# A row-by-row norm on ScalarE and earlier adds in a graph layer on one core

## The chip, the cores and the metric

The kernel runs on one core of one Trainium2 chip. The metric is the device time of one execution in microseconds (us), as the median of several runs. A core has five engines with a program each: TensorE (PE; its weight loads are shown as PEld), VectorE (DVE), ScalarE (ACT), GpSimd (POOL) and SyncE (SP), which here only issues transfers. They wait for each other by semaphores.

## The reference

One layer of a graph network: 6250 nodes of 64 features, 206250 edges sorted by their target `dst`.

```python
h = jnp.maximum(_layernorm(x, axis=-1), 0.0)
msg = h[src] + edge_attr_64
agg = jax.ops.segment_sum(msg, dst, num_segments=6250)
x = x + (jax.nn.relu(agg @ W1 + b1) @ W2 + b2)
```

## The kernel before, in words

**The norm (the head).** x lies in SBUF as `xl`, 49 rows of 64 elements on each of 128 partitions, in two parts of 24 and 25 rows (`parts`, split at `XA`). Mean, centred x, variance and `rs`, one over the root, are worked out for both parts. Then `norm_h(k)` (L550) takes the maximum with 0 and scales, in one VectorE instruction over the whole part (L552), and stores it on SP into `table`, a copy of h in HBM (L553); `norm_copy(k)` (L555) copies the part on ScalarE into `h2`, the operand of the later matmuls, and `norm_low(k)` adds its low half there.

**Most edges: counts.** For windows of edges TensorE multiplies two one-hot arrays (`hot_lo`, `hot_key`, made by VectorE in `count`, L837, for three steps at once in two buffers) into `pc` in PSUM: how often each node of a table of 128 x 49 occurs as a source (L847). ScalarE moves these counts into a ring in SBUF (L850). `multiply` (L866) then multiplies h2 with the counts into `pv`, the sums of h per target node, and `add_products` (L879) adds them into `agg` (called `sums` in the profile). `pc` has two buffers, so the matmuls of a step wait for ScalarE's reading of two steps before.

**The other work.** The edges' own features are summed with one-hot matmuls into `bank` (`chunk_hot` L422, `chunk_sum` L434) and placed into `pv` (L450). For 18 groups of edges at the end of the list h is not counted but gathered: POOL gathers rows of `table` with indirect transfers that add onto the edge features (`pfeat`, L296); `sum_groups` (L477) sums a pair of groups, `place_groups` (L489) puts it into place, ScalarE copies it to `sum_p` (L491), and `add_sums` (L461) adds it on VectorE, in two instructions at addresses read at run time, into `agg`. Nodes whose sums are complete go through the layers: `mlp_hidden` multiplies agg with W1 into `ph` (L915, ScalarE's `hid` L917), `mlp_product` gives `po` (L922), then the residual is added (L933) and stored.

**The order.** It is written out by hand: each engine gets its instructions in the order in which the Python code emits them. After the head there are 23 blocks of 14 steps (block b, step s, number n = 14 b + s). Each step emits one `count`, for block b - 1 a part of `multiply`, and what is due: the dictionary `before` gives things for a step number, and `at(n, f)` puts f to the end of step n. `mlp` puts ph of one set of nodes to step 8 of a block, and of another to step 11 where there is one (`LAYERS`). A pair of groups that is summed at step n (only at `GROUPS`, steps 0, 1, 2 and 4) is placed at the next step in `PLACED` that is at least 2 later; `add_later` puts its adds at least 5 steps behind that (3 in the last block), at any step but 10 (`ADDED`). The conditions on agg are kept by semaphores: an instruction that writes agg at a run-time address waits for matmuls before it in the order that read agg, and matmuls wait for adds before them.

**The part of the head around the change.** `norm_scale` gives rs; `unpack_pair(0)`, `chunk_rows`, `chunk_columns` (it ends with ScalarE's `cols`, L360), `turn_pair(0)` (it ends with ScalarE's `keys`, L705, which the first hot_lo waits for), two of `by_quarters` (ScalarE's `src_p`, L632), `norm_h(0)`, `norm_copy(0)`, `chunk_index`, gathers of `dstq` and words on POOL, `load(0)` (two transfers of features on SP), `norm_h(1)`, `norm_copy(1)`, `load(1)`. At step 4 `chunk_nodes(0)` works on the gathered dstq on VectorE (L378) and `chunk_turn(0)` turns it on TensorE (`pdst`, L386); step 3 has the last `by_quarters`, step 7 the `seek` on ScalarE (`inrow`, L312).

Of the kernel before, what the change touches and what calls it, by code (L numbers as in the profile page):

```python
# [14 lines left out]
AF = mybir.ActivationFunctionType  # L15
# [4 lines left out]
P = 128  # L20
# [45 lines left out]
HI = 49  # L66
# [6 lines left out]
XA = 24  # L73
# [3 lines left out]
NW = 23  # L77
# [33 lines left out]
KR = 540  # L111
AHEAD = 16
OPENING_US = 15.0


@with_exitstack
def gnn_kernel(ctx: ExitStack, tc: tile.TileContext, x, src_t, dst_t, dst_g, edge, w1, b1, w2, b2, out):
    nc = tc.nc
# [12 lines left out]
    table = dram.tile([HI * P, D], F32, name="table")  # L131
# [209 lines left out]
    def chunk_rows(c0, c1):  # L341
        s = starts[:, c0:c1]
        nc.vector.tensor_scalar(s, s, float(G * P * J - CE), None, op0=OP.min)
        nc.vector.tensor_copy(starts_i[:, c0:c1], s)
# [59 lines left out]
    def load(u):  # L404
        if u >= len(units):
            return
        _, c, n = units[u]
        at = nc.values_load_multi_w_load_instructions(
            starts_i[0:1, c:c + n], engines=[mybir.EngineType.SP], min_val=0, max_val=G * P * J - CE,
            skip_runtime_bounds_check_because="sums of edges before, at most that by a min")[1]  # L410
        feats[u] = [work.tile([P, CT, D], F32, name="feat", bufs=4) for _ in range(n)]
        for k in range(n):
            nc.sync.dma_start(feats[u][k].rearrange("p (q k) d -> p q (k d)", q=JQ),
                              edge[ds(at[k], CE), :].rearrange("(q p k) d -> p q (k d)", p=P, k=JP))
# [86 lines left out]
    xh = xl[:, :HI, :]  # L501
    stat = late.tile([P, 4, HI], F32, name="stat")
    mean, var, rs, t = (stat[:, k, :] for k in range(4))
    parts = [(0, XA), (XA, HI)]
# [14 lines left out]
    def wide(a, h0, h1):  # L519
        return a[:, h0:h1].unsqueeze(2).to_broadcast([P, h1 - h0, D])  # L520
# [21 lines left out]
    def norm_scale():  # L542

        nc.vector.reciprocal(rs, t)
        nc.vector.tensor_tensor(t, rs, rs, op=OP.mult)
        nc.vector.tensor_tensor(t, t, var, op=OP.mult)
        nc.vector.tensor_scalar(t, t, -0.5, 1.5, op0=OP.mult, op1=OP.add)
        nc.vector.tensor_tensor(rs, rs, t, op=OP.mult)

    def norm_h(k):  # L550
        h0, h1 = parts[k]
        nc.vector.scalar_tensor_tensor(xh[:, h0:h1], xh[:, h0:h1], 0.0, wide(rs, h0, h1), op0=OP.max, op1=OP.mult)  # L552
        nc.sync.dma_start(table.rearrange("(l h) d -> l h d", l=P)[:, h0:h1, :], xh[:, h0:h1])  # L553

    def norm_copy(k):  # L555
        h0, h1 = parts[k]
        nc.scalar.activation(h2[:, h0:h1, :D], xh[:, h0:h1], AF.Copy)
# [66 lines left out]
    def by_quarters(t0, t1):  # L624
        rows = src_s.bitcast(F32)
        for t in range(t0, t1):
            own = slice(t * QP, (t + 1) * QP)
            px = ps.tile([P, 512], F32, tag="pv", name="psrcq")[:, :GP * PK]
            for b in range(PQ):
                nc.tensor.matmul(px, spread[own, b].rearrange("p a c -> p (a c)"), rows[own, :, b, :],  # L630
                                 start=(b == 0), stop=(b == PQ - 1))
            nc.scalar.activation(src_p[:, :, t], px.rearrange("p (g k) -> p g k", k=PK), AF.Copy)  # L632
# [43 lines left out]
    def unpack(i0, n, p, base):  # L676
        words = words_of.pop(i0)
        klo = late.tile([P, 2, SLOTS], I32, name="klo")
        khi = late.tile([P, 2, SLOTS], I32, name="khi")
        nc.vector.tensor_scalar(klo[:p, :n], words[:p, :n], P - 1, None, op0=OP.bitwise_and)  # L680
        nc.vector.tensor_scalar(khi[:p, :n], words[:p, :n], LO_BITS, None, op0=OP.logical_shift_right)
        klof = late.tile([P, 2, SLOTS], BF16, name="klof")
        nc.scalar.activation(klof[:p, :n], klo[:p, :n], AF.Copy)
        khif = late.tile([P, 2, SLOTS], BF16, name="khif")
        nc.vector.tensor_tensor(khif[:p, :n], khi[:p, :n], base.unsqueeze(2).to_broadcast([p, n, SLOTS]),
                                op=OP.subtract)
        unpacked[i0] = klof, khif
# [4 lines left out]
    def turn(i0, n, p, cols):  # L692
        klof, khif = unpacked.pop(i0)
        pk = ps.tile([P, 2, 2, P], F32, tag="po", name="pk", bufs=1)
        for i in range(n):
            nc.tensor.matmul(pk[:, 0, i, :p], klof[:p, i, :], identb[:p, :p], start=True, stop=True)
            nc.tensor.matmul(pk[:, 1, i, :p], khif[:p, i, :], identb[:p, :p], start=True, stop=True)
        pk = pk.rearrange("s k i p -> s k (i p)")
        for a, z, col in cols:
            while a < z:  # L700
                m = min(z - a, KR - col % KR)
                assert col + m - KR <= opened[0], (i0, col, m, opened[0])
                for c in range(col, col + m):
                    at_col[c % KR] = c
                nc.scalar.activation(keys[:, :, col % KR:col % KR + m, :],  # L705
                                     pk[:, :, a:a + m].unsqueeze(3).to_broadcast([P, 2, m, 2]), AF.Copy)
                a, col = a + m, col + m
        rows = min(p, NWIN - i0 * P) if i0 < IC and n == 1 else p
        kept[i0] = khif, n, rows
# [7 lines left out]
    def unpack_pair(i0):  # L717
        n = min(2, IC - i0)
        unpack(i0, n, P, nbase[:, i0:i0 + n])

    def turn_pair(i0):
        n = min(2, IC - i0)
        end = min(n * P, NWIN - i0 * P)
        mid = min(max((SB + 1) * BT - NX - i0 * P, 0), end)
        turn(i0, n, P, [(a, z, i0 * P + a + o) for a, z, o in ((0, mid, 0), (mid, end, NX)) if a < z])
# [266 lines left out]
    by_quarters(0, 1)  # L992
    norm_scale()
    unpack_pair(0)
    chunk_rows(0, 2 * RC)
    chunk_columns(0, 2, "pc", 2)
    turn_pair(0)
    by_quarters(1, 3)
    norm_h(0)
    norm_copy(0)  # L1000
# [3 lines left out]
    fetch_dst(1)  # L1004
    fetch_pair(4)
    load(0)
    norm_h(1)
    norm_copy(1)
    load(1)
    open_ring()  # L1010
# [62 lines left out]
    steps = [(b, s) for b in range(NW) for s in range(STEPS)]  # L1073
    first_step = [steps.index((b, 0)) for b in range(NW)]
    last = len(steps)
# [4 lines left out]
    PRODUCTS = (5, 12, 19, 26, 33, 41, HI)  # L1080
    ADDED, LOADED = 10, 2
    LAST, LATE = (5, 10), 9
    GROUPS, PLACED = (0, 1, 2, 4), (1, 2, 4, 5)
    ready = []
    queued = set()
# [21 lines left out]
    def add_later(n):  # L1107

        upto = h_next

        def f():
            add_sums()
            for m in range(NW, NB):
                if (upto >= G or (start[m + 1] + 30) * (E / N) <= upto * P * J) and m not in queued:
                    queued.add(m)
                    ready.append(m)
        at(n, f)

    for n, (b, s) in enumerate(steps):
        for f in before.get(n, []):  # L1120
            f()
        count(b, s)
        if b >= 1 and s < len(PRODUCTS):
            multiply(b - 1, PRODUCTS[s])
        if b >= 1 and s == PLACES:
            for u in places[b - 1]:
                chunk_place(u)
        if b >= 1 and s == (ADDED if b < NW - 1 else LATE):
            add_products(b - 1)
            if b - 1 > SB:  # L1130
                ready.append(b - 1)
        k = n - (first_step[SB + 1] + ADDED + 1)
        if 0 <= k < 3 * -(-NX // 4) and k % 3 == 0:
            add_seconds(k // 3 * 4)
            if k // 3 == -(-NX // 4) - 1:
                ready[:0] = range(SB + 1)
        if s == LOADED or b == NW - 2 and s == STEPS // 2:
            for m in ready[:len(LAYERS)] if b < NW - 1 else ready + [NW - 2, NW - 1]:
                if m not in xs:
                    residual(m)  # L1140
        if b == NW - 1 and s == STEPS // 2:
            for m in range(NW, NB):
                if m not in queued:
                    residual(m)
        if s in (LAYERS if b < NW - 1 else LAST) and ready and ready[0] in xs:
            mlp(ready.pop(0), n)
        for f in later.pop(n, []):
            f()
        if n >= 3:
            if h_next < G and s in GROUPS and fetched.get(h_next + 1, 1e9) + LAND_US <= clock(n):  # L1150
                features_h(h_next)
                n_placed = next((k for k in range(n + 2, last) if b == NW - 1 or steps[k][1] in PLACED), last)
                at(n_placed, place_groups, h_next)
                h_next += GB
                add_later(next((k for k in range(n_placed + (3 if b == NW - 1 else 5), last) if steps[k][1] != ADDED), last))
            if n == 3:
                pool[0] = clock(n - 1) + OPENING_US
            pool_until(clock(n) + LAND_US)
# [142 lines left out]
```

## Time and profile before

| | before |
|---|---|
| median of 3 runs | 478.37 us (478.1 to 478.75) |
| profiled execution, its own time | 481.19 us |
| its span, first to last instruction | 479.4 us |
| TensorE busy | 418.0 us, 87% of the span |
| VectorE busy | 417.1 us, 87% |
| ScalarE busy | 369.0 us, 77% |
| GpSimd busy | 355.8 us, 74% |
| mean granted clock of TensorE | 0.981 |

The profile is one execution, recorded by the hardware. In a timeline a line gives start and length in us, engine, source line, operation, output and inputs by the program's names, shape, how many were merged (x), and in brackets how long the engine sat idle before it and what released it. A line of the waits gives who waited for whom, the sum in us, how many times, and the longest. Busy shares are means over stages with different limits; the head ends at about 60 us, and the blocks' rhythm after that is some 17 to 18 us.

### The profile page before, as it was taken

The page shows a single profiled execution, that of the slowest core. Times are in us where ns is not written, and L with a number is a line of the kernel's source. Part 1 is how long each engine was busy: PE and PEld are TensorE (multiplying, and loading weights), DVE is VectorE, ACT ScalarE, POOL GpSimd, SP SyncE. Part 2 cuts the span into 40 slices and gives each one's busy share as a digit, 9 for nine tenths or more (in the row PEclk, how much of TensorE's full clock was granted, in tenths as well). Part 3 has the DMA queues.
Part 4 walks back from the last instruction along what each step waited for, and adds up shares of the span by engine and source line. Part 5 has one row for each costly group of instructions (what it writes and reads, how often), then busy time and mean ns, then how long its engine had stood idle before and what let it go on. Part 6 is the DMA issues. An engine that isn't in the chain of part 4 may idle for free.

```text
span 479.4 us, 17275 instructions
## 1 busy us (share of the span) xinstructions
PE 418.0 (87%) x7339; PEld 373.4 (78%) x7340; DVE 417.1 (87%) x562; ACT 369.0 (77%) x611; POOL 355.8 (74%) x223
## 2 busy tenths in 40 slices
PE   2147698999988999999979999999999999999974
PEld 2136597887887898898878988988988988888964
DVE  7788989889999899989699899898998899898740
ACT  3636889978878789889868789787887788688650
POOL 7777888898888888888888888888888888500000
PEclk9999699999999999999989999999999999999998
DMA  9949457468367668576674694596695694474330
GB/s 236 219 148 313 118 147 167 98 175 218 66 161 193 155 172 228 121 202 166 152 189 114 178 246 105 142 248 142 147 241 123 158 225 106 130 210 133 91 83 16
DMA packets 120050, 77.70 MB, mean 162 GB/s; under 512 B 32448, under 2 KB 118400, under 8 KB 119744
## 3 DMA queue, kind: packets, MB, share of 16 engines
q1 hardware_dynamic: 97452, 67.13, 47.9%
q0 software_dynamic: 22288, 8.67, 14.1%
q8 instruction: 59, 0.97, 0.9%
q10 hardware_dynamic: 228, 0.75, 0.5%
q14 instruction: 23, 0.19, 0.1%
HBM read 72.53 MB, written 3.99 MB: 160 GB/s over the span
## 4 chain that ended last, share of the span: by engine, by line
PE 70%; ACT 11%; DMA 8%; DVE 6%; issue 3%; POOL 1%; DVEq 0%; ACTq 0%; POOLq 0%
PE pv L866 27%; PE pc L847 23%; PE bank L434 10%; ACT counts L850 8%; PE po L922 3%; DMA rows<-in_dst_g,row_i 2%; DMA feat<-in_edge 2%; PE pv L450 2%; DVE hot_key L837 2%; DMA dstq<-in_dst_g,cols_i 2%; DVE hot_lo L837 1%; POOL rows L296 1%; PE ph L915 1%; ACT junk L673 1%; DMA firsts_i<-in_dst_g 1%
## 5 line engine op out<-in xcount | busy, mean ns | idle before, releaser
L296 POOL DMA_INDIRECT pfeat<-table,src_p x144 | 299.7, 2081 | 45.0 <-issue 39.9
L850 ACT ACTIVATE counts<-pc 128x882 fp32r<-128x882 f32 x322 | 286.2, 916 | 56.7 <-PE pc L847 49.9
L847 PE MATMUL pc<-hot_key,hot_lo 128*128 128x147 bf16 x1932 | 180.8, 232 | 27.1 <-ACT counts L850 16.9
L866 PE MATMUL pv<-counts,h 128*128 128x252 f32 x1127 | 171.6, 292 | 0.1
L847 PEld LDWEIGHTS <-hot_lo 128*128 128x128 bf16 x1932 | 132.2, 100 | 49.2 <-issue 22.9
L837 DVE TENSOR_TENSOR hot_key<-iota_key,keys 128x2664 bf16<-128x2664 bf16 (+1 forms) x109 | 165.5, 1519 | 0.0
L837 DVE TENSOR_TENSOR hot_lo<-iota_lo,keys 128x2304 bf16<-128x2304 bf16 (+1 forms) x109 | 145.6, 1336 | 21.4 <-PE pc L847 18.1
L866 PEld LDWEIGHTS pv<-counts,h 128*128 128x128 f32 x1127 | 143.6, 190 | 0.4 <-ACT counts L850 0.3
L434 PE MATMUL bank<-feat,hot 128*21 128x64 f32 x3288 | 62.4, 225 | 0.2 <-DMA feat<-in_edge 0.2
L434 PEld LDWEIGHTS bank<-feat,hot 128*21 128x21 f32 x3288 | 49.9, 103 | 9.5 <-issue 0.7
L422 DVE TENSOR_TENSOR hot<-rel,iota 128x504 f32<-128x504 bf16 x69 | 46.5, 673 | 0.0
L296 POOL DMA_INDIRECT words<-packed,first_i x15 | 21.2, 1413 | 4.6 <-issue 4.3
L296 POOL DMA_INDIRECT rows<-in_dst_g,row_i x15 | 18.7, 1248 | 5.2 <-issue 3.0
L437 ACT ACTIVATE by_node<-bank 128x128 f32<-128x128 f32 x69 | 19.5, 283 | 2.1 <-PE bank L434 1.9
L879 DVE TENSOR_TENSOR sums<-sums,pv 128x126 f32<-128x126 f32 (+2 forms) x31 | 10.0, 343 | 11.0 <-PE pv L866 10.9
L917 ACT ACTIVATE hid<-ph,b1s 128x252 f32<-128x252 f32 (+2 forms) x25 | 11.6, 463 | 9.0 <-PE ph L915 9.0
L922 PE MATMUL po<-w2s,hid 128*126 128x64 f32 (+2 forms) x100 | 17.1, 295 | 1.2 <-ACT hid L917 1.2
L922 PEld LDWEIGHTS po<-w2s,hid 128*126 128x126 f32 (+2 forms) x100 | 13.8, 198 | 4.3 <-ACT hid L917 2.0
L915 PE MATMUL ph<-sums,w1s 128*128 128x252 f32 (+2 forms) x50 | 16.2, 405 | 0.5 <-ACT y L928 0.4
L450 PE MATMUL pv<-select,by_node 128*64 128x42 f32 x274 | 12.6, 235 | 0.0
L450 PEld LDWEIGHTS pv<-select,by_node 128*64 128x64 f32 x274 | 9.9, 137 | 3.1
L312 ACT ACTIVATE inrow<-rows,nhalf 128x256 bf16<-128x256 int32 x15 | 7.4, 499 | 5.2 <-DMA rows<-in_dst_g,row_i 5.2
(201 smaller groups left out, 244.4 us busy)
## 6 DMA issues: line engine op xcount, KB each, us to landing
feat<-in_edge SPq DMA_DIRECT2D x137, 384.0 KB
pfeat<-in_edge SPq DMA_DIRECT2D x18, 256.0 KB
pfeat<-table,src_p POOLq DMA_INDIRECT x144, 4.4
xl<-in_x SPq DMA_DIRECT2D x2, 768.0 KB
xs<-in_x SPq DMA_DIRECT2D x23, 63.0 KB
out_y<-y SPq DMA_DIRECT2D x23, 63.0 KB
dstn<-in_dst_g SPq DMA_DIRECT2D x1, 1024.0 KB
table<-xl SPq DMA_DIRECT2D x1, 800.0 KB
```

Source lines behind the costliest of these rows:

```text
L296: nc.gpsimd.indirect_dma_start(out=rows, out_offset=None, in_=source, in_offset=bass.IndirectOffsetOnAxis(ap=index, axis=0), compute_op=op)
L422: nc.vector.tensor_tensor(hot_of[u][:, :n].rearrange("p c j w -> p (c j) w"), rel[:, c:c + n].rearrange("p c q k -> p (c q k)").unsqueeze( ...
L434: nc.tensor.matmul(bank[q * QP:q * QP + WQ, i * D:(i + 1) * D], hot[:, i, j, :], feat[i][:, j, :], start=(k == 0), stop=(k == JP - 1))
L437: nc.scalar.activation(by_node[u][:, :n].rearrange("p c d -> p (c d)"), bank[:, :n * D], AF.Copy)
L450: nc.tensor.matmul(pvs[b][0][i * D:(i + 1) * D, a:a + CN], of[:, i, :], select, start=False, stop=False)
L837: nc.vector.tensor_tensor(hot[:, :n].rearrange("p t (m o) -> p t m o", o=2), iota_k.rearrange("p (m o) -> p m o", o=2).unsqueeze(1).to_bro ...
L847: nc.tensor.matmul(pc[:, k, m * K:(m + 1) * K], hot_lo[:, j, :], hot_key[:, j, :K], start=True, stop=True)
L850: nc.scalar.activation(ring[:, (2 * b + half) % 3, :, i * ST * V:(i + 1) * ST * V].rearrange("p h (k m) -> p h k m", k=2), pc[:, :, :ST // ...
L866: nc.tensor.matmul(pv.rearrange("p (k n) -> p k n", k=2), h2[:, h, :], of[:, :, h, :], start=(h == 0), stop=(h == HI - 1))
L915: nc.tensor.matmul(ph[:, :n], w1s, agg[:, start[b]:start[b + 1]], start=True, stop=True)
L917: nc.scalar.activation(outs[b][:, :n], ph[:, :n], AF.Relu, bias=b1s)
L922: nc.tensor.matmul(po[:pairs[b], k, :], outs[b][:, k:2 * pairs[b]:2], w2s, start=True, stop=True)
```

## The change

Two things. In the head the second part of `norm_h`, one VectorE instruction of 128 x 1600, becomes 25 activations on ScalarE of 128 x 64, one for each row: Relu with the row's column of `rs` as the scale. The first 12 are put behind `unpack_pair(0)`, that is ahead of `cols`, the other 13 behind `turn_pair(0)`, that is ahead of the two `by_quarters`. The store of this part stays where it was in SP's order (`norm_store`). And `add_later` puts a pair's adds at least 3 steps behind its placing, at step 6 or 7 of a block alone (in the last block at any step but 9).

```diff
+MID = XA + 12
...
+    def norm_rows(a, z):
+        for h in range(a, z):
+            nc.scalar.activation(xh[:, h], xh[:, h], AF.Relu, scale=rs[:, h:h + 1])
+
+    def norm_store(k):
+        h0, h1 = parts[k]
+        nc.sync.dma_start(table.rearrange("(l h) d -> l h d", l=P)[:, h0:h1, :], xh[:, h0:h1])
...
     norm_scale()
     unpack_pair(0)
+    norm_rows(XA, MID)
     chunk_rows(0, 2 * RC)
     chunk_columns(0, 2, "pc", 2)
     turn_pair(0)
+    norm_rows(MID, HI)
     by_quarters(1, 3)
     norm_h(0)
     norm_copy(0)
...
     load(0)
-    norm_h(1)
+    norm_store(1)
     norm_copy(1)
     load(1)
...
+    ADDS = (6, 7)
...
-                add_later(next((k for k in range(n_placed + (3 if b == NW - 1 else 5), last) if steps[k][1] != ADDED), last))
+                add_later(next((k for k in range(n_placed + 3, last) if steps[k][1] in ADDS or steps[k][0] == NW - 1 and
+                                steps[k][1] != LATE), last))
```

In step numbers, of the nine pairs of adds five move: those at (block, step) (6, 7), (8, 7), (15, 7) and (17, 7) by one step to step 6, and that at (10, 9) by two steps to (10, 7). In block 10 ph stands at step 8.

## The prediction

> **What bounds the kernel now.** I read the page first, then the chain of work that ended last in order of time, then the waits summed over the span, and last the timelines of single engines around the places that the diff touches. From the page, the span and the chain's shares by engine:
>
> ```profile
> span 479.4 us, 17275 instructions
> ...
> PE 70%; ACT 11%; DMA 8%; DVE 6%; issue 3%; POOL 1%; DVEq 0%; ACTq 0%; POOLq 0%
> ```
>
> The reader is to see that the chain lies on TensorE for most of the span: an edit on VectorE or ScalarE counts only where TensorE waits for it. The profiled execution took 481.19 us, 1.8 us more than its span and 2.8 us more than the median of the three timed runs, 478.37 us. The sum below is made against 481.19 us and then carried over to 478.37 us as a difference. About 0.2%, 0.96 us, can be told from no change here.
>
> The two parts of the change touch two places. The first is one long wait of VectorE, from the summed waits:
>
> ```profile
> DVE sums L461 <- PE ph L915: 4.4, 1, 4.4
> ```
>
> It happens once. The timeline of VectorE shows where, and that of TensorE what it did there:
>
> ```profile
> 233.48 0.67 DVE L422 TENSOR_TENSOR hot<-rel,iota 128x504 f32<-128x504 bf16 x1
> 238.54 0.43 DVE L461 TENSOR_TENSOR sums<-sums,sum_p 64x52 f32 x2 [4.39 <-PE ph L915]
> 239.00 1.36 DVE L837 TENSOR_TENSOR hot_lo<-iota_lo,keys 128x2304 bf16<-128x2304 bf16 x1
> 240.27 1.54 DVE L837 TENSOR_TENSOR hot_key<-iota_key,keys 128x2664 bf16<-128x2664 bf16 x1
> ```
>
> ```profile
> 234.37 0.56 PE L847 MATMUL pc<-hot_key,hot_lo 128*128 128x147 bf16 x6
> ...
> 236.26 0.87 PE L434 MATMUL bank<-feat,hot 128*21 128x64 f32 x48
> ...
> 237.80 0.63 PE L915 MATMUL ph<-sums,w1s 128*128 128x252 f32 x2
> 238.27 0.55 PE L847 MATMUL pc<-hot_key,hot_lo 128*128 128x147 bf16 x6
> 241.87 0.56 PE L847 MATMUL pc<-hot_key,hot_lo 128*128 128x147 bf16 x6 [3.05 <-DVE hot_key L837]
> 242.36 1.37 PE L434 MATMUL bank<-feat,hot 128*21 128x64 f32 x48
> ```
>
> L461 is the pair of adds of gathered sums placed at step 9 of block 10. It waits for the matmul ph of step 8, which reads the same array, and ph stands in TensorE's queue behind everything until 237.80. VectorE sits idle for 4.39 us, so hot_lo and hot_key of the next three steps come late, and TensorE, done with 238.27, waits 3.05 us for them. So here VectorE sets the end, and what it waited for was TensorE itself.
>
> **The adds, part by part.** With the change the pairs of adds stand at step 6 or 7 of a block, the last block apart. In the instruction order of the two kernels six of the nine keep their place on VectorE and three pass one small instruction; one of these three is the pair above, which goes ahead of the "hot" at 233.48 and, in the program, ahead of ph. Among the semaphores it waits for TensorE's is gone, and ph waits for the adds instead. From ScalarE's timeline there:
>
> ```profile
> 233.09 0.21 ACT L491 ACTIVATE sum_p<-placed 128x52 f32<-128x52 f32 x1 [0.23 <-PE placed L489]
> ...
> 238.19 0.92 ACT L850 ACTIVATE counts<-pc 128x882 fp32r<-128x882 f32 x1
> ```
>
> sum_p is done at 233.09 + 0.21 = 233.30, before VectorE is free at about 233.5; the adds take 0.43, "hot" 0.67, so VectorE is through at 234.6. ph at 237.80 is far behind them. hot_lo then needs the buffer of two openings earlier, which TensorE frees with the counts at 234.37 + 0.56 = 234.93. hot_lo and hot_key take 1.36 + 1.54 with some overlap: ready near 237.8, before TensorE ends 238.27 + 0.55 = 238.82. What is late next is the bank of counts: ScalarE reads it from 238.19 to 239.11. So the matmuls of 241.87 start near 239.15, 2.7 us sooner.
>
> There is more. From the table by stretches (busy time and count of each engine, then the granted clock, the share of the DMA engines and GB/s):
>
> ```profile
> 244.00:246.00 2.00, 2.00 (x16) 2.00 (x16) 1.46 (x2) 0.79 (x3) 1.70 (x2) 0.51 0.72 195
> ```
>
> TensorE came back slow: the same 48 matmuls took 0.87 at 236.26 and 1.37 at 242.36, and the granted clock was 0.51 from 244 to 246.
>
> [...]
>
> The whole is best read from block to block. These are ph of block 10 (above, 237.80), of block 11, and of two later blocks with no other extra work between them:
>
> ```profile
> 259.03 0.63 PE L915 MATMUL ph<-sums,w1s 128*128 128x252 f32 x2
> ...
> 366.98 0.63 PE L915 MATMUL ph<-sums,w1s 128*128 128x252 f32 x2
> ...
> 384.02 0.63 PE L915 MATMUL ph<-sums,w1s 128*128 128x252 f32 x2
> ```
>
> Block 10 to 11 takes 259.03 - 237.80 = 21.23; the later pair 384.02 - 366.98 = 17.04. The difference is 4.2, the direct count 2.7 plus the slow matmuls. I take 4.1 us off. If the moved adds found their cover gone (VectorE late by more than the 0.3 us that it waits for the buffer anyway), it would cost that lateness alone; all nine pairs together are 18 adds of about 0.2.
>
> **The rows in the head.** The timelines of ScalarE and VectorE there:
>
> ```profile
> 17.79 0.50 ACT L312 ACTIVATE inrow<-rows,nhalf 128x256 bf16<-128x256 int32 x1
> ...
> 28.64 0.23 ACT L540 ACTIVATE stat<-stat 128x49 f32<-128x49 f32 x1
> ...
> 31.99 0.41 ACT L683 ACTIVATE klof<-klo 128x256 bf16<-128x256 int32 x1
> 34.48 0.23 ACT L360 ACTIVATE cols<-pcols 128x2 f32<-128x2 f32 x2 [2.08 <-PE pcols L358]
> 35.02 1.02 ACT L705 ACTIVATE keys<-pk 128x1024 bf16<-128x1024 f32 x1 [0.31 <-PE pk L697]
> 36.87 0.20 ACT L632 ACTIVATE src_p<-psrcq 128x36 int32<-128x36 f32 x1 [0.82 <-PE psrcq L630]
> 37.75 0.21 ACT L632 ACTIVATE src_p<-psrcq 128x36 int32<-128x36 f32 x1 [0.68 <-PE psrcq L630]
> 37.85 2.90 ACT L557 ACTIVATE h<-xl 128x1536 fp32r<-128x1536 f32 x2
> 40.65 1.70 ACT L850 ACTIVATE counts<-pc 128x882 fp32r<-128x882 f32 x2
> ```
>
> ```profile
> 34.96 1.82 DVE L552 SCALAR_TENSOR_TENSOR xl<-xl,stat 128x1600 f32<-128x1600 f32 x1
> ...
> 44.27 0.42 DVE L378 TENSOR_SCALAR dstq<-dstq,cols 128x384 f32<-128x384 int32 x1 [1.87 <-DMA dstq<-in_dst_g,cols_i]
> ...
> 47.29 1.54 DVE L837 TENSOR_TENSOR hot_key<-iota_key,keys 128x2664 bf16<-128x2664 bf16 x1
> ```
>
> One VectorE instruction (the second of L552, 1.82 us at 34.96) is replaced by 25 activations of 128x64 on ScalarE, 12 ahead of "cols" and 13 behind "keys". The store of the second part of the table leaves on SP behind them, near 39.4 us by the sum below, and SP's next loads behind that store; I cost both at nothing, since their readers come steps later, and if that cover is gone it is at most the same 1.65 us as below. Price of one row: 128x49 took 0.23 with no per-partition operand; 64 adds 0.01; the operand (rs, one column) adds what L312 with nhalf shows over L683 without, both 128x256: 0.50 - 0.41 = 0.09. So 0.33 long. Neighbours overlap: 37.75 lasts 0.21 but 37.85 starts 0.10 after it.
>
> So a row takes 0.235 of ScalarE, 25 rows 5.9 us. Bounds: 0.14 if the operand is free, 0.33 if nothing overlaps; I take 0.235, from the nearest rows. The waits named in the brackets between 31.99 and 40.65 are 2.08 + 0.31 + 0.82 + 0.68 = 3.9, and four overlaps that a waiting engine lost give 0.35 more: 4.25 us of cover. The first counts (40.65) come 5.9 - 4.25 = 1.65 us later. The queue behind the rows: cols moves from 34.48 to about 35.2, keys from 35.02 to 35.3, then src_p, the two copies at 37.85, the counts.
>
> Who waits for that? On TensorE, and in ScalarE's next row:
>
> ```profile
> 41.60 0.90 PE L847 MATMUL pc<-hot_key,hot_lo 128*128 128x147 bf16 x6 [0.98 <-ACT counts L850]
> ...
> 44.28 0.92 PE L847 MATMUL pc<-hot_key,hot_lo 128*128 128x147 bf16 x6
> 45.49 0.91 PE L386 MATMUL pdst<-ident,dstq 128*128 128x128 f32 x3 [0.30 <-DVE dstq L379]
> ...
> 48.88 0.95 PE L847 MATMUL pc<-hot_key,hot_lo 128*128 128x147 bf16 x12 [1.00 <-ACT counts L850]
> ```
>
> ```profile
> 47.18 1.71 ACT L850 ACTIVATE counts<-pc 128x882 fp32r<-128x882 f32 x2 [0.25 <-PE pc L847]
> ```
>
> The third group of pc (41.60) is held by the first counts, and what stands behind it goes with it. But two later steps are held by others, which takes up part of the shift. pdst at 45.49 waits for VectorE's dstq, and dstq for its gather; the pc at 44.28 would have let it go at 45.20: 0.3 us of slack. At 48.88 TensorE waits for hot_key (47.29 + 1.54 = 48.83), while the counts that free its bank end near 47.18 + 0.9 = 48.08: 0.8 us more.
>
> So 1.65 - 0.3 - 0.8 = 0.55 us remain, lost. The 1.82 us saved on VectorE bring nothing by themselves: hot_lo is then held by keys, and VectorE stands 1.87 us before dstq in any case. What could come of it is an earlier gather, by POOL's timeline:
>
> ```profile
> 31.36 0.97 POOL L296 DMA_INDIRECT rows<-in_dst_g,row_i  x1 [0.30 <-issue]
> ...
> 35.69 1.91 POOL L296 DMA_INDIRECT dstq<-in_dst_g,cols_i  x1 [0.30 <-issue]
> ```
>
> The gather at 35.69 took 1.91 where the one at 31.36 took 0.97, and it ended 0.82 after L552 did (36.78). Without L552 it ends 0.95 us sooner. [...] In my sum it is worth nothing, as TensorE is by then 1.3 us late from ScalarE.
>
> Sum: 481.19 - 4.1 + 0.55 = 477.64 for a profiled execution; 478.37 - 4.1 + 0.55 = 474.8 us for the median.
>
> **The rivals.**
> 1. The rows hide wholly (0.14 each, 3.5 us under 4.25 us of cover). Then the earlier dstq counts: pdst comes up to 0.3 sooner, hot_key up to 0.9, of which the counts at 48.08 allow some 0.5. 478.37 - 4.1 - 0.5 = 473.8 us. For it: the waits are long. Against: the price by L312. Chance 0.16.
> 2. The clock in the head. By stretches:
>
> ```profile
> 52.00:54.00 2.00, 1.22 (x9) 1.03 (x9) 1.97 (x4) 2.00 (x6) 1.70 (x2) 0.50 0.00 0
> 60.00:62.00 2.00, 2.00 (x56) 1.67 (x55) 1.97 (x5) 1.07 (x2) 1.70 (x2) 0.59 0.86 230
> ```
>
> TensorE runs at about half clock for some 10 us there; it is busy for 1.22 of the first two microseconds shown and all of the last two, so I take half of the stretch, 5 us, as bound by it. If the shifted work keeps the clock up there, that half runs up to twice as fast: 2.5 us less, 472.3 us. [...] Chance 0.10.
> 3. The rows cost 0.33 each, nothing overlapping: 8.25 - 4.25 - 1.1 = 2.9 us lost, 478.37 - 4.1 + 2.9 = 477.2 us. Chance 0.10.
> 4. The slow matmuls behind the pause stay, whatever made them slow; then the adds bring 2.7 us alone: 478.37 - 2.7 + 0.55 = 476.2 us. Against it is the clock's row, right behind the pause. Chance 0.03. [...]
> 5. The adds don't do what they should: the wait of 4.39 is met again in another place, as ph now waits for the adds and they for sum_p. Then only the head counts: 478.9 us. Against it are the 3.8 us between the adds and ph. Chance 0.06.
> 6. Slower: the rows are dearer still. The loss is 25 rows less 5.35 us of cover and slack; it eats the 4.1 us at 0.38 a row and makes the kernel slower by over 0.96 us from 0.42 on: 479.4 us or more. That would need each row to wait for the one before; the order lists no such wait. Chance 0.06.
>
> **How the numbers follow.** The forecast, 474.8 us, has 0.49; its own range is 473.9 to 475.9. The range from rival 2 to rival 3, 472.3 to 477.2, leaves out 0.12. Faster: 0.49 + 0.16 + 0.10 + 0.10 + 0.03 = 0.88; within 0.2%: rival 5, 0.06; slower: rival 6, 0.06.
>
> **What would show it.** In the changed kernel's waits, "sums <- PE ph" should be gone, and ph of blocks 10 and 11 should stand about 17.1 us apart with a granted clock of 1.00 between. The new activations should show about 0.33 each, 0.235 from start to start, the first counts near 42.3, pc of step 6 near 49.4, ph of block 10 about 0.5 later than 237.80. I am wrong on the adds if blocks 10 and 11 stand over 18 us apart, and on the head if ph of block 10 comes before 237.3 or after 239.5.

## The result and the profile after

| | time, us | ratio to the kernel before, 95% |
|---|---|---|
| before, 7 runs beside it | 478.75 (478.1 to 480.17) | |
| after | 475.65 (474.77 to 477.71) | 0.9931 [0.9911, 0.995] |
| after, profiled execution | 477.71 | |
| forecast: median, profiled execution | 474.8, 477.64 | 0.9925 |

The change makes the kernel 0.7% faster, by an interval of 0.5 to 0.9%: 3.1 us by the medians, 3.3 by the ratio, where 3.55 was forecast. Ranges and ratios leave out executions that took over 1.5% longer than the fastest of the same kernel, here one of 2083.96 us. The page of the kernel after: its span, and the shares of the chain that ended last.

```profile
span 475.9 us, 17297 instructions
...
PE 71%; ACT 15%; DMA 7%; DVE 3%; issue 3%; POOL 1%; DVEq 0%; ACTq 0%; POOLq 0%
```

The span is 3.5 us shorter, and the chain still lies on TensorE; ScalarE's share rose from 11% to 15%. Lines of the code move by 1 to 9 (L461 is now L462, L837 is L846, L847 is L856, L850 is L859, L915 is L924).

**The adds.** Block 10 in VectorE's and in TensorE's timeline of the kernel after (start, length, engine, line, operation, in brackets the idle time before it and what ended it), and the row of the table by stretches that answers to the one of before (1.00 at its end is the granted clock, ahead of the DMA engines' share and GB/s):

```profile
234.15 0.42 DVE L462 TENSOR_TENSOR sums<-sums,sum_p 64x52 f32 x2
234.60 0.69 DVE L423 TENSOR_TENSOR hot<-rel,iota 128x504 f32<-128x504 bf16 x1
235.59 1.36 DVE L846 TENSOR_TENSOR hot_lo<-iota_lo,keys 128x2304 bf16<-128x2304 bf16 x1 [0.31 <-PE pc L856]
```

```profile
238.43 0.63 PE L924 MATMUL ph<-sums,w1s 128*128 128x252 f32 x2
...
239.80 0.55 PE L856 MATMUL pc<-hot_key,hot_lo 128*128 128x147 bf16 x6 [0.34 <-ACT counts L859]
240.28 0.87 PE L435 MATMUL bank<-feat,hot 128*21 128x64 f32 x48
...
255.66 0.63 PE L924 MATMUL ph<-sums,w1s 128*128 128x252 f32 x2
```

```profile
244.00:246.00 2.00, 2.00 (x54) 1.85 (x43) 1.88 (x3) 1.81 (x3) 1.70 (x2) 1.00 0.88 268
```

The adds stand at 234.15, ahead of "hot", and wait for nothing. hot_lo follows at 235.59, where it stood at 239.00 before. TensorE, which had stood still for 3.05 us, now waits 0.34 us, and for ScalarE. Its clock stays at 1.00 and the 48 matmuls of "bank" keep to 0.87. From ph of block 10 to that of block 11 it is 255.66 - 238.43 = 17.23 us, where it was 21.23: 4.00 us came from here.

**The head.** ScalarE's timeline, and the 25 rows as one group (count, shortest, median and longest in ns):

```profile
32.77 2.96 ACT L558 ACTIVATE xl<-xl,stat 128x64 f32<-128x64 f32 x12
35.63 0.20 ACT L361 ACTIVATE cols<-pcols 128x2 f32<-128x2 f32 x2
35.74 1.01 ACT L714 ACTIVATE keys<-pk 128x1024 bf16<-128x1024 f32 x1
36.64 3.21 ACT L558 ACTIVATE xl<-xl,stat 128x64 f32<-128x64 f32 x13
39.74 0.28 ACT L641 ACTIVATE src_p<-psrcq 128x36 int32<-128x36 f32 x2
39.90 2.92 ACT L566 ACTIVATE h<-xl 128x1536 fp32r<-128x1536 f32 x2
42.70 1.70 ACT L859 ACTIVATE counts<-pc 128x882 fp32r<-128x882 f32 x2
```

```profile
L558 ACT ACTIVATE xl<-xl,stat x25: 332/343/347, 32.8 to 39.5; 128x64 f32<-128x64 f32 x25
```

The rows fill what were waits. Behind them cols, keys, src_p, the copies and the first counts follow with no gap. TensorE, VectorE and POOL there:

```profile
43.66 0.90 PE L856 MATMUL pc<-hot_key,hot_lo 128*128 128x147 bf16 x6 [2.95 <-ACT counts L859]
...
49.64 1.39 PE L856 MATMUL pc<-hot_key,hot_lo 128*128 128x147 bf16 x12 [0.26 <-ACT counts L859]
```

```profile
30.27 0.46 DVE L545 RECIPROCAL stat<-stat 128x49 f32<-128x49 f32 x1
...
42.41 0.40 DVE L379 TENSOR_SCALAR dstq<-dstq,cols 128x384 f32<-128x384 int32 x1
```

```profile
36.26 0.95 POOL L297 DMA_INDIRECT dstq<-in_dst_g,cols_i  x1 [2.54 <-DVE cols L366]
```

TensorE now waits 2.95 us for the first counts, 0.98 before. POOL's gather took 0.95 instead of 1.91 and ends at 36.26 + 0.95 = 37.21 (37.60 before), and VectorE doesn't wait for the gathered dstq any more (1.87 before).

For the following comparisons the head needs a common mark, as its beginning varies between executions ahead of all that was edited (the mark taken here stands at 27.59 us in e4's profile and at 30.27 in this one). I take the reciprocal of `norm_scale`, 30.27 above. Before it stood at

```profile
29.80 0.46 DVE L544 RECIPROCAL stat<-stat 128x49 f32<-128x49 f32 x1
```

so 0.47 us of what is later in this execution's head lay ahead of everything that was edited. Less these 0.47, cols stands at 35.16, keys at 35.27 and the first counts at 42.23, as foreseen (35.2, 35.3, 42.3).

### The profile page after: what moved, and what is told of

Read it like the earlier page. It is cut to its first block, busy times and chain, and to the rows that moved or that the text cites. A ratio compares the mean times of both kernels' runs of the same rounds, so it can differ in the third digit from the quotient of the medians.

```text
span 475.9 us, 17297 instructions
## 1 busy us (share of the span) xinstructions
PE 414.9 (87%) x7339; PEld 370.7 (78%) x7340; DVE 415.9 (87%) x561; ACT 373.7 (79%) x636; POOL 344.9 (72%) x223
## 3 DMA queue, kind: packets, MB, share of 16 engines
HBM read 72.53 MB, written 3.99 MB: 161 GB/s over the span
## 4 chain that ended last, share of the span: by engine, by line
PE 71%; ACT 15%; DMA 7%; DVE 3%; issue 3%; POOL 1%; DVEq 0%; ACTq 0%; POOLq 0%
PE pv L875 27%; PE pc L856 24%; PE bank L435 10%; ACT counts L859 9%; DMA feat<-in_edge 3%; PE po L931 3%; DMA rows<-in_dst_g,row_i 2%; PE pv L451 2%; ACT junk L682 1%; ACT xl L558 1%; PE ph L924 1%; DMA firsts_i<-in_dst_g 1%; PE bank L478 1%; POOL rows L297 1%; PE psrcq L639 1%
## 5 line engine op out<-in xcount | busy, mean ns | idle before, releaser
L297 POOL DMA_INDIRECT pfeat<-table,src_p x144 | 295.1, 2050 | 45.8 <-issue 39.6
L859 ACT ACTIVATE counts<-pc 128x882 fp32r<-128x882 f32 x322 | 286.1, 917 | 52.9 <-PE pc L856 46.0
L856 PE MATMUL pc<-hot_key,hot_lo 128*128 128x147 bf16 x1932 | 179.6, 231 | 25.8 <-ACT counts L859 18.9
L856 PEld LDWEIGHTS <-hot_lo 128*128 128x128 bf16 x1932 | 131.1, 99 | 47.7 <-issue 26.3
L846 DVE TENSOR_TENSOR hot_lo<-iota_lo,keys 128x2304 bf16<-128x2304 bf16 (+1 forms) x109 | 145.7, 1337 | 25.0 <-PE pc L856 21.1
L846 DVE TENSOR_TENSOR hot_key<-iota_key,keys 128x2664 bf16<-128x2664 bf16 (+1 forms) x109 | 165.5, 1518 | 0.0
L435 PE MATMUL bank<-feat,hot 128*21 128x64 f32 x3288 | 61.2, 222 | 1.7 <-DVE fl L743 0.9
L435 PEld LDWEIGHTS bank<-feat,hot 128*21 128x21 f32 x3288 | 48.5, 101 | 11.1 <-DMA feat<-in_edge 1.5
L297 POOL DMA_INDIRECT words<-packed,first_i x15 | 17.9, 1193 | 4.6 <-issue 4.3
L297 POOL DMA_INDIRECT rows<-in_dst_g,row_i x15 | 16.9, 1126 | 5.5 <-issue 3.0
L888 DVE TENSOR_TENSOR sums<-sums,pv 128x126 f32<-128x126 f32 (+2 forms) x31 | 10.0, 343 | 11.2 <-PE pv L875 11.1
L924 PE MATMUL ph<-sums,w1s 128*128 128x252 f32 (+2 forms) x50 | 16.2, 405 | 0.5 <-ACT y L937 0.4
```

The source lines that it names most:

```text
L297: nc.gpsimd.indirect_dma_start(out=rows, out_offset=None, in_=source, in_offset=bass.IndirectOffsetOnAxis(ap=index, axis=0), compute_op=op)
L435: nc.tensor.matmul(bank[q * QP:q * QP + WQ, i * D:(i + 1) * D], hot[:, i, j, :], feat[i][:, j, :], start=(k == 0), stop=(k == JP - 1))
L846: nc.vector.tensor_tensor(hot[:, :n].rearrange("p t (m o) -> p t m o", o=2), iota_k.rearrange("p (m o) -> p m o", o=2).unsqueeze(1).to_bro ...
L856: nc.tensor.matmul(pc[:, k, m * K:(m + 1) * K], hot_lo[:, j, :], hot_key[:, j, :K], start=True, stop=True)
L859: nc.scalar.activation(ring[:, (2 * b + half) % 3, :, i * ST * V:(i + 1) * ST * V].rearrange("p h (k m) -> p h k m", k=2), pc[:, :, :ST // ...
L924: nc.tensor.matmul(ph[:, :n], w1s, agg[:, start[b]:start[b + 1]], start=True, stop=True)
```

## The experiments

Kernels that ran on one occasion share their runs of the kernel before: e1 to e4 (479.46 us), e5 to e8 (479.33 us), e9 and e10. All times are medians.

**e1 and e2: each half alone.** In e1 the diff of the adds is kept and the head is as before; in e2 the reverse.

```diff
e1, against after: the head as before
-    norm_rows(XA, MID)
...
-    norm_rows(MID, HI)
...
-    norm_store(1)
+    norm_h(1)
e2, against after: the pairs of adds as before
-    ADDS = (6, 7)
...
-                add_later(next((k for k in range(n_placed + 3, last) if steps[k][1] in ADDS or steps[k][0] == NW - 1 and
-                                steps[k][1] != LATE), last))
+                add_later(next((k for k in range(n_placed + (3 if b == NW - 1 else 5), last) if steps[k][1] != ADDED), last))
```

> The adds at step 6 or 7 alone; the norm as before. Theory (the two parts simply add up): ph of block 10 stands where it stood before (237.8 us, within 0.2), ph of block 11 comes 4.0 us sooner, and all that follows stays 4.0 us sooner; the median is 4.0 us under before, 0.8%. Rival (the slow matmuls behind the pause have another cause): ph of block 11 comes 2.7 us sooner and the granted clock stays near 0.5 for some microseconds there. Rival (the rows on ScalarE bring part of the gain): less than 3.4 us under before.

> The 25 rows on ScalarE alone; the adds as before, with the wait at step 9 of block 10. Theory: the first ph comes 0.6 us later than before, as in the changed kernel, the wait of 4.4 us stays, and the median is 0.3 to 0.6 us over before, which is at the edge of what can be told; no gain in any stage. Rival (the head gains in the median and only the profiled executions differ by chance): 0.5 us or more under before.

e1: 475.21 us, ratio 0.9893 [0.9865, 0.9921]. e2: 480.24 us, 1.0014 [0.9991, 1.0036]. The adds are the whole gain, and the rows bring none; what they cost, 0.7 us by e2, can't be told from nothing. The wait of block 10 goes with the adds: in e2 it is still there, by the summed waits. In e1 ph of block 10 stood at 238.35, 0.55 us behind the kernel before and not within 0.2 as expected, with a longer wait in the head ahead of it (3.38 us for dstq, 1.87 before; see the table further down).

```profile
DVE sums L462 <- PE ph L924: 4.3, 1, 4.3
```

**e3: no norm of the second part.** The rows are left out and nothing takes their place, so the second part of h is neither cut off at 0 nor scaled.

```diff
-    norm_rows(XA, MID)
...
-    norm_rows(MID, HI)
```

> The adds as in the changed kernel, and the maximum and scale of the second part of x left out altogether, on both engines (its output is another one for that reason). It shows what the head gives at most when that work costs nothing on any engine. Theory: hot_lo starts once keys is there, 0.6 us sooner than before; the gather of dstq is not held up by L552 and ends 0.9 us sooner; the first ph comes 0.5 to 1.5 us sooner than before and the median is 4.5 to 5.5 us under before. Rival (the work was hidden in the head anyway, since VectorE waits 1.87 us for dstq): the first ph within 0.2 us of before, the median 4.0 us under.

473.93 us, 0.9876 [0.9848, 0.9903]. With this work gone from both engines the kernel gains 1.3 us on e1 by the medians, and the intervals overlap. So there is little to be had from wherever the norm is put.

**e4: the rows split.** 8 rows ahead of cols, 9 behind keys, the last 8 in one VectorE instruction of 128x512 ahead of the store.

```diff
-MID = XA + 12
+MID = XA + 8
+TOP = MID + 9
...
+    def norm_rest():
+        nc.vector.scalar_tensor_tensor(xh[:, TOP:], xh[:, TOP:], 0.0, wide(rs, TOP, HI), op0=OP.max, op1=OP.mult)
...
-    norm_rows(MID, HI)
+    norm_rows(MID, TOP)
...
+    norm_rest()
     norm_store(1)
```

> The adds as in the changed kernel; of the 25 rows 8 go to ScalarE ahead of cols, 9 behind keys, and the last 8 stay in one VectorE instruction of 128x512 where L552 stood. 17 rows of 0.24 are 4.1 us, within the 4.25 us of waits. Theory: the first counts come within 0.3 us of before (40.65), hot_lo starts behind keys near 36.2, and the first ph comes 0.3 to 0.8 us sooner than before, so the median is 4.3 to 4.8 us under before, more than the change gave. Rival (any row on ScalarE delays the chain of keys and counts): the first ph 0.2 us later than before or more.

474.72 us, 0.9891 [0.986, 0.9923], as e1. VectorE's, ScalarE's and POOL's timelines in its head:

```profile
27.59 0.46 DVE L546 RECIPROCAL stat<-stat 128x49 f32<-128x49 f32 x1
...
30.44 1.74 DVE L554 SCALAR_TENSOR_TENSOR xl<-xl,stat 128x1536 f32<-128x1536 f32 x1
...
32.59 0.68 DVE L562 SCALAR_TENSOR_TENSOR xl<-xl,stat 128x512 f32<-128x512 f32 x1
...
42.18 0.42 DVE L380 TENSOR_SCALAR dstq<-dstq,cols 128x384 f32<-128x384 int32 x1 [2.77 <-DMA dstq<-in_dst_g,cols_i]
```

```profile
38.67 1.68 ACT L863 ACTIVATE counts<-pc 128x882 fp32r<-128x882 f32 x2
```

```profile
30.13 2.88 POOL L298 DMA_INDIRECT rows<-in_dst_g,row_i  x1 [0.30 <-ACT src_p L645]
...
34.56 1.05 POOL L298 DMA_INDIRECT dstq<-in_dst_g,cols_i  x1 [0.30 <-DVE hot_lo L850]
```

With 17 rows the first counts come 11.08 us behind the reciprocal (10.85 before, 12.43 with 25 rows). But dstq is waited for again, 2.77 us, and the first ph comes 0.1 us later than before and not 0.3 to 0.8 sooner. The timeline suggests why: a gather of `rows` ahead took 2.88 us and ended at 33.01, 0.83 us behind the end of L554 (32.18). So the gather of dstq, though short itself, ended 8.02 us behind the reciprocal, no earlier than the 7.70 to 7.84 of four profiles with the norm as before; with 25 rows it ended at 6.93 to 6.94 in three. On e1 nothing is won that can be told on this occasion.

**e5 and e6: other steps for the adds.** Both are e1 with another step, so the head is as before; the adds stand at step 9 alone, behind ph, or at step 8, the step of ph, where they are emitted ahead of it.

```diff
-    ADDS = (6, 7)
+    ADDS = (9,)      # e5
+    ADDS = (8,)      # e6
```

> The norm as before; every pair of adds at step 9 of a block (the last block apart), where one pair stood before. Theory (an add placed behind ph makes VectorE wait until TensorE gets to ph): seven blocks, 6, 8, 10, 13, 15, 17 and 20, have ph at step 8 and an add behind it, so seven waits of about 4.4 us on VectorE where before had one, each worth about 4.0 us: 24 us more than before, near 503 us. Rival (the wait of before came from block 10 alone, by what was queued there): one or two such waits, within 5 us of before.

> The norm as before; every pair of adds at step 8 (the last block apart), where the code emits them ahead of ph of the same step. Theory (only the order against ph counts): no wait of VectorE for ph, ph waits for the adds instead, and the time is that of the adds at step 6 or 7 within 0.3 us, 4.0 us under before. Rival (ph, now right behind the adds, waits for them): TensorE waits up to 1 us for the adds in each of seven blocks, and the time is 1 to 5 us over that of the adds at step 6 or 7.

e5: 491.45 us, 1.0256 [1.0221, 1.0291]. e6: 474.79 us, 0.9918 [0.9888, 0.9948]. The summed waits of e5, and VectorE's rows behind them:

```profile
DVE sums L461 <- PE ph L915: 18.4, 7, 4.4
```

```profile
163.22 0.43 DVE L461 TENSOR_TENSOR sums<-sums,sum_p 64x52 f32 x2 [1.24 <-PE ph L915]
...
200.25 0.43 DVE L461 TENSOR_TENSOR sums<-sums,sum_p 64x52 f32 x2 [2.52 <-PE ph L915]
...
238.38 0.43 DVE L461 TENSOR_TENSOR sums<-sums,sum_p 64x52 f32 x2 [4.35 <-PE ph L915]
...
295.64 0.43 DVE L461 TENSOR_TENSOR sums<-sums,sum_p 64x52 f32 x2 [4.11 <-PE ph L915]
...
334.88 0.43 DVE L461 TENSOR_TENSOR sums<-sums,sum_p 64x52 f32 x2 [1.23 <-PE ph L915]
...
372.34 0.43 DVE L461 TENSOR_TENSOR sums<-sums,sum_p 64x52 f32 x2 [2.50 <-PE ph L915]
...
428.53 0.43 DVE L461 TENSOR_TENSOR sums<-sums,sum_p 64x52 f32 x2 [2.45 <-PE ph L915]
```

The wait is made at will by putting the adds behind ph, seven times as expected; at step 8 it doesn't arise. So which side of ph the adds stand on decides; steps 6 and 7 can't be told from 8 (0.9893 and 0.9918, with intervals that overlap). The loss, 12.1 us, is half of what was expected, because behind two of the seven adds alone TensorE stands still for as long as in the kernel before. Two of its rows in e5:

```profile
203.98 0.56 PE L847 MATMUL pc<-hot_key,hot_lo 128*128 128x147 bf16 x6 [1.35 <-DVE hot_key L837]
...
298.98 0.56 PE L847 MATMUL pc<-hot_key,hot_lo 128*128 128x147 bf16 x6 [3.05 <-DVE hot_key L837]
```

Behind the adds of blocks 10 and 13 it stood still for 3.05 us, and its granted clock was at 0.50 within 1.1 us of its return. Behind the other five it stood still for 0.22 to 1.35 us and came back at 1.00; once, at block 17, the clock then fell to 0.50 after all, behind a further pause of 0.61 us. VectorE's waits come in three sizes, by the step number n = 14 b + 9: about 1.2 us at n = 93 and 219, 2.5 at 121, 247 and 289, 4.1 to 4.4 at 149 and 191. That is n modulo 3 = 0, 1, 2. The one-hot arrays are made for three steps at once, at n modulo 3 = 0 ahead of the adds; so at 0 VectorE comes to the adds late, and at 2 it comes early, with the next making of the arrays right behind them. This reason is read from the code's order and not tried by a run of its own; the sizes are shown.

**e7: twelve activations more.** To price a row by itself: behind every second row an activation of the same shape into a tile that nobody reads.

```diff
+    spent = late.tile([P, D], F32, name="spent")
...
             nc.scalar.activation(xh[:, h], xh[:, h], AF.Relu, scale=rs[:, h:h + 1])
+            if (h - XA) % 2:
+                nc.scalar.activation(spent, ident[:, :D], AF.Relu, scale=rs[:, h:h + 1])
```

> The changed kernel with 12 further activations of the same shape on ScalarE, one behind every second row, that read a constant and write scratch. Theory (the cover is used up by the 25 rows, and a row takes 0.24): 2.9 us more of ScalarE ahead of the first counts, all of it lost: the first counts stand 15.3 us behind the reciprocal of the norm (12.4 in the changed kernel), the first ph 2.5 to 2.9 us later, the median 2.5 to 2.9 us over that of the changed kernel. Rival (ScalarE has cover left in the head): under 1 us.

479.0 us, 1.0002 [0.9986, 1.0018]; e8 beside it 0.9942, so the twelve cost 2.2 us by the medians (0.006 x 479 = 2.9 by the ratios), where 2.5 to 2.9 was expected. By the row's price it is 12 x 0.238 = 2.86. The timelines of VectorE (the mark), ScalarE and TensorE:

```profile
28.65 0.46 DVE L545 RECIPROCAL stat<-stat 128x49 f32<-128x49 f32 x1
```

```profile
32.34 0.34 ACT L562 ACTIVATE spent<-ident,stat 128x64 f32<-128x64 f32 x1
...
43.93 1.70 ACT L863 ACTIVATE counts<-pc 128x882 fp32r<-128x882 f32 x2
```

```profile
44.90 0.90 PE L860 MATMUL pc<-hot_key,hot_lo 128*128 128x147 bf16 x6 [4.38 <-ACT counts L863]
```

The first counts stand 43.93 - 28.65 = 15.28 us behind the reciprocal, 2.85 more than with 25 rows. With the cover used up, each further row shows in full there; the first ph comes 2.5 us later.

**e8: the change once more**, on the occasion of e5 to e7.

> The changed kernel once more, beside the other three and the kernel before on the same chip. Theory (adds 4.0 us off, rows 0.3 to 0.6 us on): 3.4 to 3.7 us under before, and 0.3 to 0.6 us over the adds alone at step 8. Rival (the rows cost nothing in the median): as the adds alone, within 0.2 us; three tenths of a microsecond are under what the intervals tell apart, so the profile's positions from the reciprocal to the first ph are read beside it.

476.83 us, 0.9942 [0.992, 0.9965]; the first comparison gave 0.9931. Over the adds alone of e6, on the same occasion, it is 2.0 us by the medians and 1.2 by the ratios, where 0.3 to 0.6 was expected; the intervals overlap, so this excess is not shown, but neither is the expected size.

**e9 and e10: e4 and e1 once more**, to tell the split from the adds alone. On this occasion every kernel took 16 to 21 us longer, the kernel before too (500.69 us), for a reason that no run shows, so only comparisons within the occasion are of use.

> The split of 8 rows, 9 rows and one VectorE instruction once more, beside the adds alone on the same chip, to tell whether the split is worth having. Theory (17 rows lie within ScalarE's waits, and the gather of dstq is freed of most of L552): 4.2 to 4.8 us under before, 0.2 to 0.8 us under the adds alone, and in the profile the gather of dstq takes near 1 us and the first counts come 11.1 us behind the reciprocal. Rival (the head's gain is eaten by the landing of dstq, which goes by the transfers ahead of it): as the adds alone.

> The adds at step 6 or 7 alone once more, on the same chip as the split. Theory: 4.0 us under before, 0.2 to 0.8 us over the split; dstq lands 13 to 16 us behind the reciprocal, as in the other kernels with the norm of before, so the profiled first ph may stand anywhere between 133.2 and 136.6 us behind it.

e9: 490.45 us, 0.9825 [0.9775, 0.9875]; e10: 493.05 us, 0.9886 [0.9845, 0.9927]. The split is ahead by 0.6%. The two intervals overlap, but both have the scatter of the same runs of the kernel before in them, and the runs themselves don't overlap: the split took 489.72 to 490.72 us but for one of 502.7, the adds alone 490.76 to 496.02. On the first occasion they did overlap (e4 473.5 to 476.64, e1 473.99 to 477.64), so the split's lead is seen once in two and isn't settled. The profiles here don't explain it: in e9's, of the execution of 502.7 us, the gather took 1.34 us and the first counts came 12.90 us behind the reciprocal, where near 1 and 11.1 were expected; in e10's dstq came at 13.47, as expected, and the first ph at 138.48, where at most 136.6 was expected.

The adds alone gave 0.9893 and 0.9886, the whole change 0.9931 and 0.9942: the adds alone are ahead, at intervals that touch or overlap. All three kernels beat the kernel before by intervals that leave out 1; which of them is best isn't shown.

## Why the prediction was right

**The wait of the adds: 4.1 us foreseen, 4.0 measured.** The shift of ph between blocks 10 and 11 is the measure: 4.00 in the kernel after, 3.99 in e1, 4.00 in e3, e6 and e7, 4.01 in e4 and e8, none in e2. The steps held too: what was late next was the bank of counts by ScalarE, and the pc counted to start near 239.15 started at 239.80, in an execution that reached block 10 0.63 later. Rival 5, the wait met again elsewhere, is out.

**The slow matmuls behind the pause** went with it, as the row of the clock had it (1.00 where it was 0.51). Rival 4 is out: the 48 matmuls of "bank" behind the adds take 0.87 us, 1.37 before. A pause of 3.05 us stood ahead of the low clock in the kernel before (0.51) and twice in e5 (0.50); that the pause brought it on is the author's reading, and how long a pause that takes is shown by no run.

**The price of a row: 0.33 long and 0.235 apart foreseen, 0.343 and 0.238 measured** (the median of the 25; 39.74 - 36.64 = 3.10 for 13 rows). The first counts were to come 1.65 later and came 12.43 - 10.85 = 1.58 later, both from the reciprocal. The prices of rivals 1, 3 and 6 (0.14, 0.33 apart, 0.42 and more) are out by this and by e7.

**What remains of it: 0.55 us foreseen, 0.1 to 0.3 in this execution.** From the reciprocal, pc of step 6 starts 0.29 later than before (49.64 - 30.27 against 48.88 - 29.80), the first pv 0.22, the first ph, that of block 6, 0.11. Of the 1.58 us the wait at pdst took up 0.5, where 0.3 was foreseen, and the one at step 6 some 0.7, where 0.8 was. In e2 and e8 pc of step 6 is 0.30 and 0.28 later, and in e8, where the clock stood at 0.50 in the head as before, the first ph comes 0.50 later. That ph of block 10 was 0.63 late, where about 0.5 was foreseen, is mostly the 0.47 from ahead of the edit: the number came out for another reason. The times don't settle the term either: they put the rows at 0.7 us by e2 and at 1.2 to 2.0 by e8 over e6, none of it told from nothing.

Over all profiles the head scatters more than that:

| from the reciprocal, us | first counts | dstq on VectorE | first ph |
|---|---|---|---|
| norm as before: before | 10.85 | 14.47 | 134.70 |
| e1 | 10.84 | 15.97 | 136.55 |
| e5 | 10.88 | 13.97 | 133.77 |
| e6 | 10.74 | 13.29 | 133.22 |
| 25 rows: after | 12.43 | 12.14 | 134.81 |
| e2 | 12.43 | 12.14 | 134.90 |
| e8 | 12.43 | 12.13 | 135.20 |
| e7, 37 activations | 15.28 | 13.56 | 137.48 |
| e4, split | 11.08 | 14.59 | 134.81 |
| e3, no norm | 10.93 | 11.99 | 133.31 |

With the norm as before the first ph follows the landing of dstq, 133.2 to 136.6. With 25 rows dstq is never waited for, and the first ph follows the counts: 134.8 to 135.2. The means are 134.56 and 134.97, so the rows cost about 0.4 us on the mean and take the scatter away; neither is settled with four and three executions. The wait for dstq at its longest, in e1:

```profile
28.54 0.46 DVE L544 RECIPROCAL stat<-stat 128x49 f32<-128x49 f32 x1
...
44.51 0.42 DVE L378 TENSOR_SCALAR dstq<-dstq,cols 128x384 f32<-128x384 int32 x1 [3.38 <-DMA dstq<-in_dst_g,cols_i]
```

**The earlier gather: 0.95 us foreseen, worth nothing: right in the sum, short in size.** POOL's gather is 0.95 shorter as said (1.91 to 0.95). The data came earlier by more: VectorE could take dstq 14.47 us behind the reciprocal before, waiting for it, and at 12.14 without waiting, so at least 2.3 us sooner, and 1.15 sooner than in the earliest of the four executions with the norm as before (13.29). TensorE didn't profit, since the counts held it (2.95 above).

**Rival 2, the clock in the head: its premise came, its 2.5 us did not.** By stretches and in TensorE's timeline of the kernel after:

```profile
52.00:54.00 2.00, 0.29 (x5) 0.30 (x4) 1.82 (x6) 2.00 (x7) 1.69 (x2) 0.99 0.00 0
60.00:62.00 2.00, 0.78 (x28) 0.44 (x25) 1.93 (x6) 1.00 (x2) 1.70 (x2) 1.00 1.05 269
```

```profile
58.88 0.87 PE L435 MATMUL bank<-feat,hot 128*21 128x64 f32 x48
...
61.12 0.53 PE L435 MATMUL bank<-feat,hot 128*21 128x64 f32 x24 [0.88 <-DVE fl L743]
62.10 0.53 PE L435 MATMUL bank<-feat,hot 128*21 128x64 f32 x24 [0.45 <-DMA feat<-in_edge]
```

The clock was up in both stretches (0.99 and 1.00 instead of 0.50 and 0.59), "bank" took 0.87, and TensorE then waited 0.88 for VectorE's fl and 0.45 for features. So the half of the stretch that the rival took as bound by TensorE was not bound by it. The other profiles say the same: e8, the same program, had 0.50 in both stretches, and its first ph came only 0.39 us later from the reciprocal; in e1 the clock stood at 1.00 in every stretch from 44 to 62 us, and its first ph was the latest of those with the norm as before.

**The term that was costed at nothing:** the store and the loads behind it on SP. From the reciprocal they left 1.74 and 1.63 us later (at 39.88 and 40.93, before at 37.67 and 38.83), and no wait for these loads shows: the second bank of the head, which reads them (58.88 above), starts with no wait. The 0.45 us for features at 62.10 is another matter. The third bank reads what `load(2)` brings, and the code issues that behind the first bank, whose buffers it takes. SP's timeline of the kernel after:

```profile
56.51 6.56 SPq L414 DMA_DIRECT2D feat<-in_edge  x6
```

The wait is there in each of the five profiles of the first two occasions in which the third bank ran at full speed, 0.53 for 24 matmuls (the kernel after, e1, e3, e5, e7: 0.40 to 0.48 us), with the norm as before, moved or left out. It is in none of the five in which that bank ran slower, 1.08 to 1.49 for 48 (the kernel before, e2, e4, e6, e8). So in these ten it goes with TensorE's clock and not with the store; and it is a second reason why a faster clock there was worth so little.

Features are waited for in other places too, in every profile (in the kernel before for 0.17 us at 151.80). The place that costs most lies between ph of blocks 19 and 20. The rows of the kernel after, e8, e6 and e2, in this order (e5 waits 0.17 us there):

```profile
404.19 0.53 PE L435 MATMUL bank<-feat,hot 128*21 128x64 f32 x24 [0.25 <-DMA feat<-in_edge]
```

```profile
403.97 0.53 PE L435 MATMUL bank<-feat,hot 128*21 128x64 f32 x24 [0.60 <-DMA feat<-in_edge]
```

```profile
401.65 0.53 PE L434 MATMUL bank<-feat,hot 128*21 128x64 f32 x24 [0.77 <-DMA feat<-in_edge]
```

```profile
406.49 0.54 PE L435 MATMUL bank<-feat,hot 128*21 128x64 f32 x24 [0.35 <-DMA feat<-in_edge]
```

With the wait these two ph stand 18.39 to 19.09 us apart, the further the longer it is; without it (the kernel before, e1, e3, e4, e7) 17.99 to 18.29. So up to 1 us is lost there in some executions. How early TensorE comes doesn't decide it: e4 reaches ph of block 19 6.35 us ahead of the kernel before and doesn't wait there (it waits 0.39 us a block later), e2 is 1.19 ahead and e5 7.67 behind, and both wait. What decides it wasn't tried.

**The closeness of the profiled execution, 477.71 us against 477.64, is in part luck.** Measured in the traces, 0.47 us were lost ahead of the edit, 0.16 from there to ph of block 10 (0.55 foreseen), 4.00 won at the adds, 0.34 lost between ph of blocks 19 and 20, and 0.45 won behind them. The first, the fourth and the last of these are not in the forecast. The median came 0.85 over its forecast, and 0.38 of that is the kernel before, 478.75 beside it and not 478.37.

## What to carry to other kernels

When an engine stops for a long time at a small instruction, look whether the releaser reads or writes the same array further down another engine's queue; moving the small instruction ahead of that reader in the program won the whole pause here and the slow matmuls behind it (0.43 us of work had held up 4.0 us), and on which side it stood mattered more than by how many steps (1.0256 at step 9; 0.9893 at 6 and 7, 0.9918 at 8). Filling an idle engine's waits with many small instructions cost little here up to the sum of those waits (17 rows of 0.238 us held the first counts up by 0.23) and full price beyond it (twelve more than the 25 by 2.85), so count both before moving work. A wait that shows up only behind a change need not come from it: look whether kernels without the change have it too, as with the wait for features here, which stood in the five profiles where that bank ran at full speed and in none of the other five.

## What was not expected of the hardware

- The landing of one gather scatters: with the norm as before, anywhere from 13.3 to 16.0 us behind the reciprocal, so that the first ph came between 133.2 and 136.6; with 0.95 us less on POOL it had landed by 12.14 in each of three executions.
- In e5 the same pair of adds behind the same kind of matmul made VectorE wait 1.23 to 4.35 us, and TensorE behind it 0.22 to 3.05, by its place in the rhythm of three steps.
- The granted clock in the head isn't the program's doing alone: the kernel after and e8 are the same program, and from 60 to 62 us one had 1.00 and the other 0.50.
